# Two products change places at the head of each pass, and six idle products go before the table

## The chip, the cores and the metric

The kernel runs on one core of a Trainium2 chip. The metric is the device time of one execution in microseconds (us); of several runs the median is given. A profile is one more execution, recorded by the hardware profiler; its times count from the first instruction.

A core has five engines that run at the same time and wait for each other by semaphores: TensorE (PE in the profile, with PEld for its weight loads), VectorE (DVE), ScalarE (ACT), GpSimd (POOL) and SyncE (SP), which here issues transfers. TensorE writes to PSUM only; VectorE and ScalarE read the sums from there.

## The reference, cut to what matters

There are 128 graphs of 64 nodes with 768 features. Layer 0 is normalised, passed through a ReLU, and then a graph layer with three 768 x 768 weights is added; layer 1 is an attention layer. The change touches layer 0 alone.

```python
h = jnp.maximum(_layernorm(x, axis=-1), 0.0)
# layer 0, with adj as heads and as relations (0 or 1 here)
ctx = jnp.matmul(adj, hs @ Wadj.T + badj) / deg_c[..., None]
ctx = ctx + jnp.matmul(radj, hs @ Wrev.T + brev) / rdeg_c[..., None]
ctx = ctx + hs @ Wself.T + bself
agg = jnp.einsum('bij,bijr->bir', adj, E[rels])
rel = agg @ Wr.T + br * deg[..., None]
...                                    # the same for the reverse direction, with Wrr
x = x + ctx + rel
# layer 1
h = jnp.maximum(_layernorm(x, axis=-1), 0.0)
x = x + _L1_gnn_ref(h, adj, ...)
```

The relation part depends on x not at all: it is a count of relations per node times a small table (E times Wr and Wrr, and the biases). The kernel makes the table once and multiplies counts by it.

## The kernel before

Layer 0 goes in 32 passes (`NP`) of two row tiles of 128 rows each (`k` is 0 or 1). The products of rows and weights use a scheme for 2 x 3 by 3 x 3 blocks with 15 block products in place of 18. Each entry of `PRODUCTS` names the operand, the weight block, the PSUM bank, whether it starts that bank afresh, the block of the result, the sign, and whether counts are added as well. A product that doesn't start its bank afresh accumulates on what is in it. Pass 0 uses 18 plain products instead, while the sums of weights are being made.

```python
PRODUCTS = (
    ("f1", "g6", "a", True, "11", "+", False),
    ("f7", "g10", "b", True, "00", "-", False),
    ("a01", "b11", "d", True, "01", "+", True),
    ("f4", "b21", "a", False, "01", "-", False),
    ("a00", "g12", "b", False, "01", "-", False),
    ("f3", "g8", "c", True, "12", "-", False),
    ...
    ("a11", "g1", "b", False, "11", "+", True),
    ("f2", "g11", "a", False, "10", "+", True),
)
PLAIN = tuple((f"a{k}{j}", f"b{j}{q}", "abcdab"[2 * i + k], j == 0, f"{k}{q}" if j == 2 else None,
               "+", i > 0) for i, q in enumerate((0, 2, 1)) for k in range(2) for j in range(3))
```

A pass is a list of steps for TensorE. Each step is one fp32 matmul of the source, which the profile shows as two records; a product is six steps, so twelve records. After a product's last step VectorE adds (or subtracts) the bank to x. Each bank has one buffer.

```python
def main(p):
    ...
    def new(b):
        bank[b] = psw.tile([P, 512], F32, name=f"pw{b}")

    def counts(b, c, first=False):           # two bf16 matmuls: counts times the table
        ...
            nc.tensor.matmul(bank[b][:, :CQ], CT_T[p, k][: 3 * (e - a), i, :],       # L617
                             tabs[i][:, q * CQ : (q + 1) * CQ], ...)

    def add(b, c, sign="+"):
        ...
        if sign == "+":
            nc.vector.tensor_add(v, bank[b][:, :CQ], v)                              # L625
        else:
            nc.vector.tensor_sub(v, v, bank[b][:, :CQ])                              # L627

    def product(an, bn, b, first, c, sign, cnt):
        def step(q, s):
            if first and q == s == 0:
                new(b)
            nc.tensor.matmul(bank[b][:, :CQ], OPS[p, an][:, q, s, :],                # L633
                             bw[bn][:, (s * KQ + q) * CQ : (s * KQ + q + 1) * CQ], ...)
            if q == KQ - 1 and s == 2 and c:
                if cnt:
                    counts(b, c)
                add(b, c, sign)
        for q in range(KQ):
            for s in range(3):
                steps.append(lambda q=q, s=s: step(q, s))

    for x in PRODUCTS if p else PLAIN:
        product(*x)

    rest_of = ["12"] if p else ["00", "10"]
    for i, c in enumerate(rest_of):
        b = "dc"[i % 2]
        steps.append(lambda b=b, c=c: (counts(b, c, True), add(b, c)))
    return steps
```

Between these steps, at given places, stands the work that makes ready the next pass (and ends the one before). A few of the entries:

```python
steps = [(0, lambda: form(p, "f5", "f6", "f3")), (10, lambda: form(p, "f10")),
         (18, lambda: form(p, "f11"))]
...
    (7, lambda: prep(n)),                    # two casts of adj on VectorE
    (13, lambda: devs(n)),
    ...
    (53, lambda: form(n, "f1")),
    ...
    (66, lambda: form(n, "f7", "f4")),
```

Ahead of pass 0 the table is made and the first operands. `degrees` is a bf16 matmul with `blkb`; `table_product` is two fp32 matmuls of 384 columns (four records), of which 0 and 1 are the two directions and 2 the biases; `operands` multiplies rows of h by the adjacency divided by the degrees.

```python
prep(0)
scaled_rows()
rd = degrees(0)                              # L518
to, mv = deviations((0,))
one_over(rd)
mean_and_relu(0, to[0], mv[0])               # h of row tile 0, on ScalarE
over_degrees(0, rd)
table_product(0)                             # L458
operands(0, 0, 0)                            # L586
table_product(1)
table_product(2)
table_copy()
operands(0, 0, 1)
...
first = [
    ...
    (30, lambda: weights_sums("w", "v")),
    (34, lambda: degrees_and_norms(1)),      # VectorE reads the degrees' PSUM tile (L520)
    (38, lambda: count_t(0, 0)),             # L572
    (45, lambda: count_t(0, 1)),
    ...]
```

Of the kernel before, what the change touches and what calls it, by code (L numbers as in the profile page):

```python
# [8 lines left out]
F32 = mybir.dt.float32  # L9
# [6 lines left out]
P = 128  # L16
# [37 lines left out]
# [7 lines that stand above are left out]
    ("a02", "g14", "a", False, "00", "-", False),  # L61
    ("f9", "g9", "b", False, "02", "+", False),
# [10 lines left out]
PLAIN = tuple((f"a{k}{j}", f"b{j}{q}", "abcdab"[2 * i + k], j == 0, f"{k}{q}" if j == 2 else None,  # L73
               "+", i > 0) for i, q in enumerate((0, 2, 1)) for k in range(2) for j in range(3))
# [58 lines left out]
def kernel(  # L133
# [45 lines left out]
    nc = tc.nc  # L179
    G, N, D = x.shape  # L180
# [9 lines left out]
    NP = NT // 2  # L190
# [35 lines left out]
    def merged(main, side):  # L226

        side = sorted(side, key=lambda e: e[0])
        i = 0
        for n, step in enumerate(main):  # L230
            while i < len(side) and side[i][0] <= n:
                side[i][1]()
                i += 1
            step()
        for _, step in side[i:]:
            step()
# [41 lines left out]
    def deviation(src, to, mv):  # L278

        st = small.tile([P, 2, 6], F32, name="st")  # L280
        for i in range(2):
            nc.vector.bn_stats(st[:, i, :], src[:, i * HALF : (i + 1) * HALF])
        nc.vector.bn_aggr(mv, st.rearrange("p a b -> p (a b)"))
        ve = small.tile([P, 1], F32, name="ve")
        nc.vector.tensor_scalar(ve, mv[:, 1:2], EPS, None, op0=OP.add)  # L285
        nc.gpsimd.tensor_tensor(to[:, 0:1], ve, mhalf, op=OP.pow)  # L286
# [67 lines left out]
    with ExitStack() as px:  # L354
        wa = px.enter_context(tc.tile_pool(name="wa", bufs=1))
        work = px.enter_context(tc.tile_pool(name="work0", bufs=2))
        psw = px.enter_context(tc.tile_pool(name="psw0", bufs=1, space=bass.MemoryType.PSUM))
# [42 lines left out]
        blkb = wa.tile([P, P], BF16, name="blkb")  # L400
# [41 lines left out]
        vals = wa.tile([P, NG, N], BF16, name="vals")  # L442
# [4 lines left out]
        def scaled_rows():  # L447
            for d in range(2):
                nc.vector.tensor_mul(es[:, d, d * NV : (d + 1) * NV],
                                     et[:, d * NB + 1 : (d + 1) * NB], ids)  # L450

        def table_product(i):

            if i == 0:
                TAB["ps"] = pss.tile([P, 2, 512], F32, name="pb")
            for hf in range(2):
                s = slice(hf * HALF, (hf + 1) * HALF)
                nc.tensor.matmul(TAB["ps"][:NROW, hf, :HALF], es[:, i, :] if i < 2 else eb,  # L458
                                 wrt[i][:, s] if i < 2 else bia[:, s],
                                 start=(i == 0), stop=(i == 2))  # L460
# [52 lines left out]
        def degrees(p):  # L513


            ds = pss.tile([P, 2, 512], F32, name="pb")[:, 0, : 4 * N].rearrange(
                "p (k d n) -> p k d n", k=2, d=2)
            nc.tensor.matmul(ds, blkb, AB[p], start=True, stop=True)  # L518
            rd = work.tile([P, 2, 2, N], F32, name="rd", bufs=1)
            nc.vector.tensor_scalar(rd, ds, 1.0, None, op0=OP.max)  # L520
            return rd

        def one_over(rd):
            nc.vector.reciprocal(rd, rd)

        def over_degrees(p, rd):

            for d in range(2):
                nc.vector.tensor_mul(rts[p % 2][:, :, 1 - d, :], ADF[p][:, :, d, :], rd[:, :, d, :])
# [47 lines left out]
        def operands(p, k, q):  # L577


            t = 2 * p + k  # L580
            ps = pss.tile([P, GT, 512], F32, name="pb")
            for i in range(2):
                kb = 2 * q + i
                for g in range(GT):
                    s = slice(g * N, (g + 1) * N)
                    nc.tensor.matmul(ps[:, g, i * 3 * N : (i + 1) * 3 * N],  # L586
                                     H0[t][s, kb * P : (kb + 1) * P],
                                     rts[p % 2][s, k].rearrange("p s n -> p (s n)"),
                                     start=True, stop=True)

            a = OPS[p, f"a{k}{q}"] = (
                work.tile([P, KQ, 3, P], F32, name="oq") if (k, q) == (1, 1) else
                work.tile([P, KQ, 3, P], F32, name="op", bufs=17))
            nc.scalar.copy(a.rearrange("p h s (g n) -> p g (h s) n", g=GT),  # L594
                           ps[:, :, : 6 * N].rearrange("p g (x n) -> p g x n", n=N))
# [8 lines left out]
        def main(p):  # L604

            bank = {}
            steps = []

            def new(b):
                bank[b] = psw.tile([P, 512], F32, name=f"pw{b}")  # L610

            def counts(b, c, first=False):
                k, q = int(c[0]), int(c[1])
                if first:
                    new(b)
                for i, (a, e) in enumerate(PARTS):
                    nc.tensor.matmul(bank[b][:, :CQ], CT_T[p, k][: 3 * (e - a), i, :],  # L617
                                     tabs[i][:, q * CQ : (q + 1) * CQ],
                                     start=(first and i == 0), stop=True, skip_group_check=True)

            def add(b, c, sign="+"):
                k, q = int(c[0]), int(c[1])
                v = X[2 * p + k][:, q * CQ : (q + 1) * CQ]
# [9 lines that stand above are left out]
                    nc.tensor.matmul(  # L633
                        bank[b][:, :CQ], OPS[p, an][:, q, s, :],
                        bw[bn][:, (s * KQ + q) * CQ : (s * KQ + q + 1) * CQ],
                        start=(first and q == s == 0), stop=(q == KQ - 1 and s == 2),
                        skip_group_check=True)
# [5 lines that stand above are left out]
                    for s in range(3):  # L643
                        steps.append(lambda q=q, s=s: step(q, s))

            for x in PRODUCTS if p else PLAIN:
                product(*x)

            rest_of = ["12"] if p else ["00", "10"]
# [4 lines that stand above are left out]
# [22 lines left out]
        def deviations(ts):  # L676
            to = [small.tile([P, 2], F32, name="rn") for t in ts]
            mv = [small.tile([P, 2], F32, name="mv") for t in ts]
            for i, t in enumerate(ts):
                deviation(X[t], to[i], mv[i])  # L680
            return to, mv
# [5 lines left out]
        prep(0)  # L687
        scaled_rows()
        rd = degrees(0)
        to, mv = deviations((0,))  # L690
        one_over(rd)
        mean_and_relu(0, to[0], mv[0])
        over_degrees(0, rd)
        table_product(0)
        operands(0, 0, 0)
        table_product(1)
        table_product(2)
        table_copy()
        operands(0, 0, 1)
# [98 lines left out]
        for p in range(NP):  # L798
            merged(main(p), beside(p) if p else first)
# [436 lines left out]
```

## Time and profile before

| What | Value |
|---|---|
| Median of 3 runs | 2499.7 us (2497.94, 2499.7, 2507.48) |
| The profiled execution | 2494.1 us span, 35435 instructions |
| PE busy | 2458.7 us, 12108 instructions |
| DVE busy | 1998.9 us, 4105 instructions |
| ACT busy, POOL busy | 1074.4 us, 449.2 us |

In a line of the costliest groups the columns are: line of the kernel, engine, operation, what it writes and what it reads, the shape, how often; then, after a bar, the busy time in us and the mean of one in ns; after a second bar, the idle time of the engine ahead of these instructions and what ended most of it. In the list of waits a line says who waited for whom, for how many us in total, how many times, and the longest. In the timeline a line has the start in us, the duration in us, the engine and line, the operation, what it writes and reads, and how many are merged into it; in brackets the idle time before it and what ended it. `pwa` to `pwd` are the PSUM banks a to d of layer 0; `pb` are PSUM tiles for operands, table and degrees. Records of matmuls overlap their successors, since matmuls are pipelined: the distance of two starts says more than a duration.

### The profile page before, as it was taken

Reading aid. Unit: us, or ns where it says so; the run is one execution under the profiler, and the core shown is the slowest. Engines: PE = TensorE matmul, PEld = TensorE weight load, DVE = VectorE, ACT = ScalarE, POOL = GpSimd, SP = SyncE. Lnnn points to the kernel's source line nnn. Section 1 sums busy time; section 2 is a strip of 40 time slices with the busy share of each in tenths; the row PEclk is TensorE's granted clock in tenths of the full one; section 3 lists DMA queues with packets and bytes.
Section 4 is the critical chain, followed back from the end, with each engine's and each line's share of the span. In section 5 each row is a group of like instructions: output and inputs, shape, how many; then the busy total and the mean of one; then the engine's idle time right before and its main releaser. Section 6 shows DMA issues by size and latency. Waiting matters only on the chain. (4 is left out here: it accounts for less than half of the span.)

```text
span 2494.1 us, 35435 instructions
## 1 busy us (share of the span) xinstructions
PE 2458.7 (99%) x12108; PEld 1724.9 (69%) x12108; DVE 1998.9 (80%) x4105; ACT 1074.4 (43%) x3591; POOL 449.2 (18%) x799
## 2 busy tenths in 40 slices
PE   8999999999999999999999999999999999999997
PEld 6888888888888888888888884444444444444445
DVE  8877777777777777777777766888888888888889
ACT  2122122122122222222222224777777777777777
POOL 1112112112111121121121121111111111111122
PEclk9999999999999999999999999999999999999999
DMA  5112112112122122122122154344444444444434
GB/s 178 55 53 106 53 60 100 53 66 93 54 72 87 53 74 85 53 79 81 54 88 72 53 174 140 94 110 111 109 104 110 104 104 104 107 113 105 104 85 100
DMA packets 116215, 224.58 MB, mean 90 GB/s; under 512 B 36554, under 2 KB 49981, under 8 KB 116034
## 3 DMA queue, kind: packets, MB, share of 16 engines
q1 hardware_dynamic: 106162, 197.50, 24.4%
q0 software_dynamic: 9728, 24.78, 6.2%
q8 instruction: 95, 1.56, 0.3%
q14 instruction: 86, 0.70, 0.1%
q10 hardware_dynamic: 144, 0.04, 0.0%
HBM read 96.07 MB, written 100.66 MB: 79 GB/s over the span
## 5 line engine op out<-in xcount | busy, mean ns | idle before, releaser
L633 PE MATMUL pwa<-weights,op 128*128 128x256 f32 x2304 | 548.9, 383 | 10.6 <-DVE x L625 8.8
L633 PEld LDWEIGHTS pwa<-weights,op 128*128 128x128 f32 x2304 | 417.4, 190 | 79.3 <-DVE x L625 17.3
L633 PE MATMUL pwb<-weights,op 128*128 128x256 f32 x1536 | 360.7, 381 | 0.0
L633 PEld LDWEIGHTS pwb<-weights,op 128*128 128x128 f32 x1536 | 289.1, 190 | 44.9 <-issue 6.7
L889 PE MATMUL pma<-weights,op_f 128*128 128x512 f32 x620 | 307.7, 593 | 0.6 <-DVE weights L916 0.6
L286 POOL TENSOR_TENSOR rn<-ve,mhalf 128x1 f32<-128x1 f32 x128 | 93.7, 732 | 948.6 <-DVE ve L285 948.5
L307 DVE TENSOR_TENSOR op<-op 128x768 f32<-128x768 f32 x248 | 241.3, 993 | 1.2
L941 ACT ACTIVATE pr<-pr 128x128 f32<-128x128 f32 x768 | 225.4, 296 | 25.3 <-DVE pr L931 25.2
L483 ACT ACTIVATE h<-x,rn 128x768 f32<-128x768 f32 x64 | 62.4, 1022 | 399.8 <-DVE rn L290 380.9
L663 ACT ACTIVATE hf<-x,rn 128x768 f32<-128x768 f32 x64 | 65.7, 1027 | 353.7 <-issue 250.1
L594 ACT COPY op<-pb 128x768 f32<-128x768 f32 x160 | 121.1, 797 | 180.9 <-PE pb L586 180.3
L889 PE MATMUL pmb<-weights,op_f 128*128 128x512 f32 x372 | 191.2, 595 | 0.0
L889 PEld LDWEIGHTS pma<-weights,op_f 128*128 128x128 f32 x620 | 111.8, 190 | 113.2 <-issue 104.3
L633 PE MATMUL pwc<-weights,op 128*128 128x256 f32 x780 | 187.0, 383 | 0.0
L633 PE MATMUL pwd<-weights,op 128*128 128x256 f32 x768 | 176.3, 379 | 0.0
L633 PEld LDWEIGHTS pwc<-weights,op 128*128 128x128 f32 x780 | 145.6, 190 | 25.2 <-issue 6.7
L665 POOL TENSOR_TENSOR x<-x,hf 128x768 f32<-128x768 f32 x64 | 136.1, 2127 | 134.9 <-ACT hf L663 134.9
L633 PEld LDWEIGHTS pwd<-weights,op 128*128 128x128 f32 x768 | 145.8, 190 | 20.0 <-issue 0.2
L586 PE MATMUL pb<-r,h 64*128 64x192 f32 x1536 | 151.8, 337 | 0.4 <-ACT h L483 0.4
L625 DVE TENSOR_TENSOR x<-pwa,x 128x256 f32<-128x256 f32 x95 | 40.0, 422 | 134.2 <-PE pwa L617 78.4
L586 PEld LDWEIGHTS pb<-r,h 64*128 64x128 f32 x1536 | 122.9, 187 | 33.9 <-issue 22.7
L941 ACT ACTIVATION_READ_ACCUMULATOR pr<-pr 128x1 f32 x768 | 144.4, 188 | 0.0
(207 smaller groups left out, 4337.6 us busy)
## 6 DMA issues: line engine op xcount, KB each, us to landing
x<-in_x_dram SPq DMA_DIRECT2D x64, 384.0 KB
h<-hf SPq DMA_DIRECT2D x64, 384.0 KB
out_dram<-x SPq DMA_DIRECT2D x64, 384.0 KB
hh<-hh SPq DMA_DIRECT2D x64, 384.0 KB
h<-h SPq DMA_DIRECT2D x64, 384.0 KB
x<-hh SPq DMA_DIRECT2D x64, 384.0 KB
out_dram<-f POOLq DMA_DIRECT2D x62, 384.0 KB, 5.0
hx<-weights SPq DMA_DIRECT2D x88, 192.0 KB
```

The source lines that it names most:

```text
L286: nc.gpsimd.tensor_tensor(to[:, 0:1], ve, mhalf, op=OP.pow)
L307: return (nc.vector.tensor_add if s1 == "+" else nc.vector.tensor_sub)(to, x, y)
L483: nc.scalar.activation(h, X[t], AF.Relu, scale=to[:, 0:1], bias=to[:, 1:2])
L586: nc.tensor.matmul(ps[:, g, i * 3 * N : (i + 1) * 3 * N], H0[t][s, kb * P : (kb + 1) * P], rts[p % 2][s, k].rearrange("p s n -> p (s n)"), ...
L594: nc.scalar.copy(a.rearrange("p h s (g n) -> p g (h s) n", g=GT), ps[:, :, : 6 * N].rearrange("p g (x n) -> p g x n", n=N))
L625: nc.vector.tensor_add(v, bank[b][:, :CQ], v)
L633: nc.tensor.matmul(bank[b][:, :CQ], OPS[p, an][:, q, s, :], bw[bn][:, (s * KQ + q) * CQ : (s * KQ + q + 1) * CQ], start=(first and q == s ...
L663: nc.scalar.activation(h, X[t], AF.Relu, scale=to[:, 0:1], bias=to[:, 1:2])
L665: nc.gpsimd.tensor_add(X[t], X[t], h)
L889: nc.tensor.matmul(bank[p, b], OPS[p, an][:, q, :], bw2[bn][:, 2 * q * CQ : 2 * (q + 1) * CQ], start=(first and q == 0), stop=(q == KQ - 1 ...
L941: nc.scalar.activation(PR[t][:, j, h, :], PR[t][:, j, h, :], AF.Copy, accum_out=to)
```

## The change

In passes 1 to 30 the first two products change places: (f7, g10) in bank b comes first, and (f1, g6) in bank a second. Pass 31 keeps the old order, and pass 0 has its own products. It is meant to let the bank in which a pass ends be read out before the next pass writes it.

Ahead of the table six bf16 products of 512 columns are issued whose result nothing reads; they are there to occupy TensorE before the first products that count. The table's second direction is moved ahead of the first operands, so that TensorE has it to do while h is being made.

```diff
-            for x in PRODUCTS if p else PLAIN:
+            later = (PRODUCTS[1], PRODUCTS[0], *PRODUCTS[2:]) if p + 1 < NP else PRODUCTS
+            for x in later if p else PLAIN:
                 product(*x)
...
         prep(0)
         scaled_rows()
         rd = degrees(0)
+
+        idle = psw.tile([P, 512], F32, name="pwa")
+        for i in range(6):
+            nc.tensor.matmul(idle, blkb, vals[:, : 512 // N, :], start=True, stop=True)
         to, mv = deviations((0,))
         one_over(rd)
         mean_and_relu(0, to[0], mv[0])
         over_degrees(0, rd)
         table_product(0)
+        table_product(1)
         operands(0, 0, 0)
-        table_product(1)
         table_product(2)
         table_copy()
         operands(0, 0, 1)
```

## Prediction

> **What bounds the kernel now.** I read the page's shares and its 40 slices first, then the waits of TensorE (PE), then the timeline at the places where PE waits. The page:
>
> ```profile
> PE 2458.7 (99%) x12108; PEld 1724.9 (69%) x12108; DVE 1998.9 (80%) x4105; ACT 1074.4 (43%) x3591; POOL 449.2 (18%) x799
> L633 PE MATMUL pwa<-weights,op 128*128 128x256 f32 x2304 | 548.9, 383 | 10.6 <-DVE x L625 8.8
> ```
>
> PE is busy for 99% of the span. The change touches layer 0 alone, which ends near 1505 us (the last record of its products starts at 1504.4). What PE lost in layer 0 is in the list of waits by PE:
>
> ```profile
> PE pwa L633 <- DVE x L625: 8.8, 30, 0.3
> PE pb L518 <- DVE ab L490: 4.2, 1, 4.2
> ...
> PE pwa L633 <- DVE x L627: 1.7, 1, 1.7
> PE pb L572 <- DVE rd L520: 0.9, 1, 0.9
> ```
>
> The reader is to see that one wait comes 30 times: the first product of a pass, written to bank a, waits for VectorE (DVE) to have added bank a into x. There are 32 passes and so 31 boundaries. Here is the boundary into pass 2 (timeline):
>
> ```profile
> 118.69 0.39 PE L617 MATMUL pwa<-tab,cntT 126*128 126x256 bf16 x2
> 118.91 0.38 PE L617 MATMUL pwd<-tab,cntT 126*128 126x256 bf16 x2
> 119.11 0.42 DVE L625 TENSOR_TENSOR x<-pwa,x 128x256 f32<-128x256 f32 x1 [2.56 <-PE pwa L617]
> 119.59 2.86 PE L633 MATMUL pwa<-weights,op 128*128 128x256 f32 x12 [0.29 <-DVE x L625]
> 122.28 2.75 PE L633 MATMUL pwb<-weights,op 128*128 128x256 f32 x12
> ```
>
> The last product of a pass (f2, g11) ends in bank a with its counts at 118.69; one more pair of counts goes to bank d; then the next pass starts in bank a again, before DVE's 0.42 us read is over. All 30 such boundaries have the same figures, and passes follow each other every 46.30 us. The boundary out of pass 0, which runs the plain products and ends in bank b, has no wait:
>
> ```profile
> 72.72 0.39 PE L617 MATMUL pwb<-tab,cntT 126*128 126x256 bf16 x2
> 72.95 0.38 PE L617 MATMUL pwd<-tab,cntT 126*128 126x256 bf16 x2
> 73.17 0.39 PE L617 MATMUL pwc<-tab,cntT 126*128 126x256 bf16 x2
> 73.34 0.42 DVE L625 TENSOR_TENSOR x<-pwb,x 128x256 f32<-128x256 f32 x1
> 73.39 2.75 PE L633 MATMUL pwa<-weights,op 128*128 128x256 f32 x12
> ```
>
> The start (timeline) shows PE at two paces:
>
> ```profile
> 7.07 0.26 PEld L458 LDWEIGHTS pb<-wrt,es 128*81 128x81 f32 x1 [0.38 <-issue]
> 7.71 0.26 PEld L458 LDWEIGHTS pb<-wrt,es 128*81 128x81 f32 x1 [0.38 <-issue]
> 9.56 1.39 PE L586 MATMUL pb<-r,h 64*128 64x192 f32 x8 [0.36 <-ACT h L483]
> 11.27 0.15 PEld L458 LDWEIGHTS pb<-wrt,es 128*81 128x81 f32 x1 [0.17 <-issue]
> 11.59 0.15 PEld L458 LDWEIGHTS pb<-wrt,es 128*81 128x81 f32 x1 [0.17 <-issue]
> 14.62 1.99 PE L633 MATMUL pwa<-weights,op 128*128 128x256 f32 x8
> 39.26 0.27 PE L572 MATMUL pb<-identb,c 128*126 128x128 bf16 x2 [0.88 <-DVE rd L520]
> ```
>
> Equal table matmuls follow each other every 0.64 us at 7.1 and every 0.32 us at 11.3.
>
> **What the Trainium skill says.** "TensorE: Matmul & The Clock Gate", Part 1: the array runs at half rate by default and at full rate once a window of about 3.4 us has been busy; the window runs free, so the moment differs from run to run. The trace agrees: 0.64 us against 0.32 us, and the operand matmuls before 10.88 change pace, some 4 us after the first table matmul at 6.38. The same page gives 512 / 1.2 = 427 ns between cold bf16 matmuls of 512 columns, which I use for the six idle products; no record of the kernel before has such a matmul. "PSUM — Partial Sum Buffer", the section on bank collisions, asks for a semaphore guard by bank: the add has to be over before PE writes the same bank. That is the wait of 119.59. "Perfetto Trace Analysis", on consistent bubbles, reads a gap that repeats on the busiest engine as too few buffers; here another order of banks does what another bank would.
>
> **The change part by part.**
>
> *1. The swap, passes 2 to 30.* In these passes the product (f7, g10) in bank b comes first and (f1, g6) in bank a second. Without a wait a product follows a pair of counts after 0.22 us (72.95 to 73.17 to 73.39 are two such steps) and takes 12 x 0.216 = 2.59 us; so from the bank d counts to the second product it would be 2.81. The trace has 122.28 - 118.91 = 3.37. The loss is 0.56 us per boundary: 0.46 of a later start (0.68 instead of 0.22), and 0.10 because the weights of a waiting first matmul are not loaded ahead (2.86 against 2.75 for the twelve). The wait list shows only 0.29 of this since the end of the counts' records overlaps the gap. Bank b was last read by DVE after the product (a11, g1): counts at 115.70, add 116.13 to 116.55, 2.5 us before it would be wanted. So the wait goes entirely: passes 2 to 30 are 29 boundaries, 29 x 0.56 = 16.2 us saved.
>
> *2. The swap in pass 1.* Pass 0 ends in bank b, with the add at 73.34 to 73.76. With bank b first, PE waits for it: start at about 73.76 + 0.06 (the lag 119.53 to 119.59) = 73.82 instead of 73.39, plus 0.10 for the first matmul: 0.53 us lost. A new wait, once.
>
> *3. Pass 31* keeps the old order, so its boundary keeps its 0.56: nothing. The 1.7 us wait of its last product is in its own DVE stream and moves along with it: nothing.
>
> *4. Does the second product meet a new wait?* It needs bank a 2.81 us after the bank d counts; the add ends at 0.62 after them. The fourth product (f4) accumulates in bank a after the add of the second: PE ends the second at about 5.5 after the counts, DVE adds until about 6.0 and PE wants the bank at 8.2. Free by 2 us. DVE before that: three sums (f5, f6, f3) from 0.9 to 3.6, the first add, two casts, f10 until 5.4. Nothing new.
>
> *5. The start.* The six products read blkb and vals (both written by 3.3 us) and fill PE from about 4.5, where the degrees matmul ends, to 4.5 + 6 x 0.43 = 7.1 us (estimate). The first table product could have started at 6.38: 0.7 us later. In return, the busy stretch begins 1.9 us earlier (4.45 instead of 6.38), so the clock should come up about 8.6 instead of 10.5. Then: table products 0 and 1, eight matmuls from 7.1, two and a half at 0.64 and the rest at 0.32, end at 10.4; the second table product fills the 0.36 us in which PE waited for h (ready at 9.51); operands 0.7 more, product 2 of the table 1.3, the second operands 0.8: first product at about 13.5 instead of 14.62, 1.1 us earlier. With the free-running window this can be 0.2 (clock as late as before) to 1.9 (clock up at 7.1). The first weights have landed by then (the trace's DMA completions: 9.96, 10.68, 12.93). But what is gained must pass 39.26, where PE waits for DVE: DVE sums w and v from 35.44 to 38.87 and only then reads the degrees. v needs b21, whose DMA completions end at 36.15 whatever PE does; v now starts at about 37.15. So at most 1.0 us gets through. I take 0.75.
>
> *Sum:* -16.2 + 0.5 - 0.75 = -16.4 us. Layer 1 has the same instructions and starts when layer 0 ends: it only moves.
>
> **The rivals.** *A. DVE takes the place.* If DVE were as late as PE, only a part of the 0.56 would come through. For it: DVE is 80% busy over the span and in pass 0 nearly all the time. Against it: in the passes concerned DVE idles 2.56 us just before the last adds (119.11), so it is released by PE at each boundary and follows it. It would make the saving 5 to 10 us: 2490 to 2495. *B. The start decides.* The six products only delay the table, the clock comes no sooner, and the gain is swallowed at 39.26: start 0 to +0.7 us instead of -0.75, total 2483.5 to 2485. *C. Only the recorded gap is saved:* 29 x 0.29 = 8.5 us, about 2491. Against it: the spacing of the starts, 3.37 against 2.81, needs no end of a record. *D. A transfer becomes the limit*: x tiles come one pass ahead, and DMA is 20% busy in the middle slices; a pass shorter by 1.2% won't reach it.
>
> **Range and chances.** 2499.7 - 16.4 = 2483.3; the three times of before lie at 2497.94, 2499.7 and 2507.48, so the median stands 1.8 over the lowest and a new median could be 3 lower or 6 higher from scatter alone. The parts worked out are good to about 1.5 us. I put 2483 with 2477 to 2490. The saving is 0.66%; 2% would be 50 us, for which no wait of layer 0 is long enough, and nothing added costs that much: faster by over 2% 0.01, within 2% 0.98, slower 0.01.
>
> **What would show it.** Passes 2 to 30 every 45.74 us instead of 46.30; the wait of pwa L633 for x L625 down from 30 times to 1, a wait of the first pwb in pass 1 of about 0.5; 0.22 us from the bank d counts to a pwb product; six matmuls of about 0.43 us from 4.5; table matmuls at 0.32 us pace before 10; first pwa product near 13.5; the matmul of 39.26 near 38.4. It would be wrong if PE waited for DVE at the second or fourth product, if the passes stayed at 46.3, or if the first products waited for weights.

## The result and the profile after

The changed kernel takes 2481.48 us (median of 4 runs, 2481.21 to 2483.03), beside 2501.7 us for the kernel before (2497.94 to 2507.48, with one run more than the three above): a ratio of 0.9918, 95% interval 0.9897 to 0.9940. So it is faster by 0.8%, clear of the scatter and within 2%. The forecast was 2483.0, in a range of 2477 to 2490. The profiled execution went from a span of 2494.1 us to 2479.7.

The list of waits by PE, kernel after (who waited for whom: us in total, times, longest):

```profile
PE pwa L633 <- DVE x L627: 1.8, 1, 1.8
PE pb L572 <- DVE rd L520: 0.9, 1, 0.9
...
PE pwa L633 <- DVE x L625: 0.3, 1, 0.3
PE pwb L633 <- DVE x L625: 0.3, 1, 0.3
```

The wait that came 30 times comes once for bank a, at the head of pass 31, and once for bank b, at the head of pass 1. The timeline of the kernel after at the head of pass 2:

```profile
118.70 0.39 PE L617 MATMUL pwa<-tab,cntT 126*128 126x256 bf16 x2
118.93 0.39 PE L617 MATMUL pwd<-tab,cntT 126*128 126x256 bf16 x2
...
119.12 0.42 DVE L625 TENSOR_TENSOR x<-pwa,x 128x256 f32<-128x256 f32 x1 [2.56 <-PE pwa L617]
119.15 2.75 PE L633 MATMUL pwb<-weights,op 128*128 128x256 f32 x12
...
121.74 0.59 PE L633 MATMUL pwa<-weights,op 128*128 128x256 f32 x2
```

From the bank d counts to the first product it is 0.22 us now, and to the second 2.81 (3.37 before). VectorE's read of bank a, 119.12 to 119.54, lies beside the product in bank b, and bank a has long been free when the second product wants it at 121.74. The first weight load of the product in bank b starts at 119.04, 0.11 us ahead of its matmul; before, load and matmul of the waiting product both started at 119.59. The heads of passes follow each other every 45.74 us (118.93 and 164.67 for passes 2 and 3, and so for all up to 31), 46.30 before. The head of pass 1 in the same timeline:

```profile
72.66 0.38 PE L617 MATMUL pwc<-tab,cntT 126*128 126x256 bf16 x2
72.83 0.42 DVE L625 TENSOR_TENSOR x<-pwb,x 128x256 f32<-128x256 f32 x1
...
73.31 2.86 PE L633 MATMUL pwb<-weights,op 128*128 128x256 f32 x12 [0.26 <-DVE x L625]
```

Here the swap made a wait: 0.65 us from the last counts to the product instead of 0.22, and 2.86 for the twelve instead of 2.75. The start of the kernel after, PE alone:

```profile
4.40 2.77 PE L696 MATMUL pwa<-vals,blkb 128*128 128x512 bf16 x6
6.96 4.07 PE L458 MATMUL pb<-wrt,es 128*81 128x384 f32 x8
10.96 0.92 PE L586 MATMUL pb<-r,h 64*128 64x192 f32 x8
...
14.10 1.99 PE L633 MATMUL pwa<-weights,op 128*128 128x256 f32 x8
...
38.75 0.27 PE L572 MATMUL pb<-identb,c 128*126 128x128 bf16 x2 [0.88 <-DVE rd L520]
```

The six idle products take 0.43 us each; the clock record puts full rate at 9.62 us (10.55 before). The first product comes 0.52 earlier than the 14.62 of before, and the matmul behind VectorE 0.51 earlier than 39.26.

So layer 0 gained what was worked out. By the 1446.06 of the first product of pass 31 (1462.29 before) the kernel was 16.23 us ahead, and so it stayed through layer 1 until its last 35 us. There it lost 1.8. Two windows of the kernel before (stretch in us, its length, then busy time and records of PE, PEld, DVE, ACT and POOL, the granted PE clock, DMA share, GB/s):

```profile
2468.00:2478.00 10.00, 5.23 (x33) 3.59 (x25) 9.72 (x22) 7.56 (x38) 2.47 (x7) 0.85 0.57 127
2478.00:2488.00 10.00, 5.33 (x63) 3.97 (x61) 9.39 (x28) 6.00 (x18) 3.21 (x3) 0.98 0.48 65
```

The stretch from the same point of the program in the kernel after, which is 16.2 us ahead there:

```profile
2452.00:2462.00 10.00, 5.23 (x23) 3.72 (x20) 9.71 (x22) 7.27 (x36) 2.47 (x7) 0.75 0.59 127
2462.00:2472.00 10.00, 7.31 (x63) 5.53 (x63) 8.03 (x25) 5.38 (x18) 2.06 (x2) 0.74 0.31 45
```

PE waits here for other engines, and the clock drops: for 3.41 us in the kernel before, for 10.24 in the kernel after. The same four matmuls in the chain of work that ended last (start, us), first before and then after:

```profile
2478.97 1.06 PE pma L1099 x4
```

```profile
2463.55 2.00 PE pma L1106 x4
```

With the clock at half they take about twice as long, VectorE waits for them (8.03 busy instead of 9.39), and the program ends later. Whether the change did that was the first question for the experiments.

### The profile page after: what moved, and what is told of

The parts are those of the page before. It is cut to its first block, busy times and chain, and to the rows that moved or that the text cites. A ratio compares the mean times of both kernels' runs of the same rounds, so it can differ in the third digit from the quotient of the medians.

```text
span 2479.7 us, 35447 instructions
## 1 busy us (share of the span) xinstructions
PE 2455.0 (99%) x12114; PEld 1727.4 (70%) x12114; DVE 1999.0 (81%) x4105; ACT 1074.7 (43%) x3591; POOL 450.1 (18%) x799
```

## The experiments

Each was run beside the kernel before on the same chip. The table has the traces' own times in us: the start of the first product; from it to the first product of pass 31; from there to a fixed VectorE instruction in layer 1 (the 1300th record from the end); from another (the 200th from the end) to the end of the span. Between those two lie 615.08 us in every one of them.

| Kernel | first product | to pass 31 | into layer 1 | last part | span |
|---|---|---|---|---|---|
| before, first profile | 14.62 | 1447.67 | 313.69 | 103.03 | 2494.1 |
| before, again | 14.45 | 1447.71 | 314.75 | 105.05 | 2497.0 |
| before, third | 14.36 | 1447.67 | 314.79 | 104.93 | 2496.8 |
| before, fourth | 16.66 | 1447.67 | 316.68 | 105.31 | 2501.4 |
| swap alone | 14.59 | 1431.96 | 313.83 | 104.71 | 2480.2 |
| start alone | 12.86 | 1448.41 | 315.51 | 105.41 | 2497.3 |
| changed kernel | 14.10 | 1431.96 | 313.76 | 104.81 | 2479.7 |
| swap from pass 2 | 14.11 | 1431.44 | 313.90 | 104.83 | 2479.3 |
| swap in pass 31 too, loads as they were | 13.17 | 1431.83 | 318.32 | 103.84 | 2482.2 |
| idle products alone | 14.31 | 1447.66 | 314.16 | 104.61 | 2495.8 |
| table moved alone | 15.17 | 1447.66 | 316.00 | 104.86 | 2498.8 |
| swap from pass 2, idle products at the end | 13.02 | 1432.01 | 315.88 | 102.81 | 2478.8 |
| and swap in pass 31, one load later | 13.62 | 1431.00 | 314.35 | 102.80 | 2476.8 |
| and idle products earlier | 12.91 | 1431.47 | 314.50 | 103.07 | 2477.0 |

**The kernel before again.** No edit.

> The kernel before, once more, to see how far its own times and its two ends scatter. My theory (the clock window runs free of the program): passes again every 46.30 us, 30 boundaries with 0.68 us from the bank d counts to the next product; the clock comes up at another moment than 10.55 us, anywhere from 9.8 to 13.2, and the last 35 us of the program have a stretch at half clock of one or more windows of 3.41 us. Rival (the change itself cost the 1.8 us at the end of the program): the kernel before always has just one window of 3.41 us at half clock in its last 35 us, as in its first profile.

Median 2499.01 of 12 runs, ratio to the kernel before 0.9995 (0.9985 to 1.0006), as it should be. Passes 46.30 us, clock up at 10.35. The windows near the end:

```profile
2469.00:2479.00 10.00, 5.23 (x26) 3.64 (x18) 9.71 (x22) 7.26 (x36) 2.48 (x7) 0.79 0.59 127
2479.00:2489.00 10.00, 7.74 (x63) 5.96 (x63) 7.81 (x24) 5.07 (x18) 2.06 (x2) 0.70 0.32 48
```

The kernel before has the half clock near its end as well, 10.24 us of it from 2474.78, and its last part takes 105.05. The rival falls: the kernel without the change loses them too, here and in its third and fourth profile (104.93 and 105.31). The first profile of before, at 103.03, was a lucky one.

**The swap alone.** The start as before:

```diff
-        idle = psw.tile([P, 512], F32, name="pwa")
-        for i in range(6):
-            nc.tensor.matmul(idle, blkb, vals[:, : 512 // N, :], start=True, stop=True)
...
-        table_product(1)
         operands(0, 0, 0)
+        table_product(1)
```

> The swap without the changed start. My theory: passes 2 to 30 every 45.74 us, a new wait of 0.53 us in pass 1, so the first product of pass 31 starts 15.7 us (29 x 0.56 - 0.53) earlier than in a kernel before whose start is the same; about 0.5 us later than in the changed kernel. Rival (the two parts help each other, the swap needs the earlier start): the first product of pass 31 comes over 1 us later than 15.7 says.

Median 2486.01 of 4 runs (2481.94 to 2490.82), ratio 0.9940 (0.9922 to 0.9958). From the first product to pass 31 it takes 1431.96 us, to the hundredth what the changed kernel takes, and 15.71 less than before: 29 x 0.56 - 0.53 = 15.71. Up to pass 31 the swap needs nothing of the start. The timed runs say less: the median lies 14.3 us under the kernel before beside it and 4.5 over the changed kernel (timed apart), where 0.5 was expected, and the four runs are spread over 8.9 us. Only the fastest of them was profiled, so what held up the others, and whether the new start prevents it, is not shown.

**The start alone.** `for x in PRODUCTS if p else PLAIN` as before, the rest as changed.

> The start without the swap. My theory: the passes stay at 46.30 us; the first product comes 0.2 to 1.2 us earlier than 14.62, by the phase of the clock window, and at most 1.0 of it passes the wait for VectorE at 39 us; over the whole kernel 0.2 to 1.0 us, too little to be seen in the medians. Rival (the six products only delay the table): first product at 14.6 or later.

Median 2498.43 of 12 runs, ratio 0.9991 (0.9983 to 1.0000). The clock was up at 7.11 us and the first product at 12.86, 1.8 us before that of the kernel before, more than the 0.2 to 1.2 expected; of this 1.0 was left at pass 31 (1461.27), and nothing at the end, as pass 31 and the last part took 1.8 and 2.4 us longer than in the first profile of before. The timeline of VectorE shows where the rest stayed:

```profile
33.69 1.76 DVE L307 TENSOR_TENSOR weights<-weights 128x1536 f32<-128x1536 f32 x1
36.09 1.76 DVE L307 TENSOR_TENSOR weights<-weights 128x1536 f32<-128x1536 f32 x1 [0.65 <-DMA tab<-tl]
37.77 0.42 DVE L520 TENSOR_SCALAR rd<-pb 128x256 f32<-128x256 f32 x1
```

These are w and v. In the kernel before v followed w at once; here VectorE waits 0.65 us for a transfer. The profile names another transfer that ended at that time; by the program the one that v needs is b21. The completion that let v go came at 35.87; the same one came at 36.15 in the first profile of before and at 35.36 in the second, so the cap itself moves by some tenths. PE stands behind it until 38.24. That is the cap that was expected.

**The swap from pass 2 on.**

```diff
-            later = (...) if p + 1 < NP else PRODUCTS
+            later = (...) if 1 < p < NP - 1 else PRODUCTS
```

> The changed kernel with the old order in pass 1, so that passes 2 to 30 alone are swapped. My theory: the wait of the first product of pass 1 goes and nothing takes its place, so from pass 1 on everything is 0.53 us earlier than in the changed kernel (if its start falls alike). Rival (VectorE sets the pace out of pass 0, where it is nearly always busy): the 0.53 us comes back as a wait later in pass 1 and the first product of pass 2 starts at the same time as in the changed kernel.

Median 2483.05 of 4 runs (2481.13 to 2485.27), ratio 0.9928 (0.9913 to 0.9943). The timeline at the head of pass 1:

```profile
72.67 0.39 PE L617 MATMUL pwc<-tab,cntT 126*128 126x256 bf16 x2
72.89 2.75 PE L633 MATMUL pwa<-weights,op 128*128 128x256 f32 x12
```

The wait is gone, and pass 31 comes 0.52 us sooner after the first product than in the changed kernel (1431.44). Nothing took its place. The medians can't show half a microsecond; the trace does.

**The swap in pass 31 too.** `... if p else PRODUCTS`, nothing else.

> The changed kernel with the swap in the last pass too. Theory one (the last pass is bound by VectorE and by the loads of layer 1's weights, not by PE): the wait of 0.56 us at the head of pass 31 goes, but (f1, g6) is now read second, so the first load that overwrites g6 starts 2.6 us later; the wait of the pass's last product for VectorE, 1.8 us in the changed kernel, grows by 0.6 to 3.2 us and layer 0 ends at the same time or up to 2.6 us later. Theory two (the wait at the head is on the path in pass 31 as in the others): layer 0 ends 0.56 us earlier and the last product's wait stays at 1.8.

Both theories missed. In pass 31 the load of b10 for layer 1 goes into the place of g6 and is issued after the first of the second product's six steps. That product now reads g6 from there: its other five steps wait for the load and multiply b10's numbers, so this kernel leaves most of the product with g6 out of pass 31. PE, kernel with the swap in all passes:

```profile
1447.59 0.59 PE L633 MATMUL pwa<-weights,op 128*128 128x256 f32 x2
1451.00 4.10 PE L633 MATMUL pwa<-weights,op 128*128 128x256 f32 x10 [2.82 <-DMA weights<-in_w_cat_dram]
1454.89 2.81 PE L633 MATMUL pwd<-weights,op 128*128 128x256 f32 x12
```

A wait of 2.82 us, and then ten records in 3.9 us instead of 2.2, since the clock fell to half from 1451.58 to 1454.99. Median 2485.58, ratio 0.9939 (0.9926 to 0.9953). That the change spares pass 31 fits this; what the wait at its head is worth it does not tell.

**The two parts of the start, each alone.** Idle products without the move of the table, and the move without the idle products; products in the old order in both.

> The six idle products alone: old order of products, table's second direction in its old place. In the timed runs of the kernel before about a third lie 5 to 6 us over the rest (near 2504 instead of 2498); with the whole new start none of twelve does. Theory one (the idle products bring the clock up early whatever the window's phase): no run near 2504, median within 1 us of the start-only kernel's 2498.4. Theory two (moving the table is what helps, since PE no longer waits for h): about a third of the runs near 2504. First product in the trace between 13.4 and 15.3 in both.

> The table's second direction ahead of the first operands, without the idle products. Theory one (the idle products are what removes the slow third of the runs): some of the runs near 2504 again, median 2499 to 2502. Theory two (moving the table is what helps): no run near 2504, median within 1 us of 2498.4. In the trace table matmuls start near 6.4 and the wait for h is gone in both.

Idle products alone: median 2499.11 of 13 runs (2496.57 to 2501.62), ratio 0.9992 (0.9984 to 1.0000); clock up at 8.93, first product at 14.31, and PE still waits 0.32 us for h. The move alone: median 2500.16 of 13 (2498.30 to 2502.20), ratio 0.9997 (0.9988 to 1.0005); clock up at 12.16, first product at 15.17. The medians order them as theory one says, and the idle products alone have no run near 2504. But the move alone has none either, which theory one did not expect. Neither part has a gain in its median that its interval sets apart from nothing; what can be seen is that runs over 2503 are gone with either of them (of 26 none; of the 25 timed beside them of the kernel before 7).

**A run near 2504, caught.** The kernel before, two more profiled executions.

> The kernel before, looked at once more, to catch one of its executions near 2504 us (17 of 60 timed ones were at 2503 or more; none of 38 with any part of the new start). Theory one (the start): the clock comes up late or the first products wait, and the first product of pass 31 starts some 5 us after 1462.2. Theory two (the passes fall into another rhythm): the passes are longer than 46.30 us by about 0.2. Theory three (the end): all is as before until 1462, and the 5 us are lost in pass 31 or in the last 35 us. If this execution is again near 2498, it says nothing of the three.

> The same kernel and the same three theories as in the run before it: a second chance to catch an execution near 2504 us.

(Of the 60 times meant there 18 are at 2503 or more, not 17.) The first took 2498.60 us, the second 2503.17. The start of the second, PE:

```profile
9.65 1.65 PE L586 MATMUL pb<-r,h 64*128 64x192 f32 x8 [0.36 <-ACT h L483]
11.23 2.85 PE L458 MATMUL pb<-wrt,es 128*81 128x384 f32 x4
...
16.66 1.99 PE L633 MATMUL pwa<-weights,op 128*128 128x256 f32 x8
```

The table matmuls at 11.23 still run at half rate (2.85 us for four against 1.52): the clock came up at 14.76, and pass 31 began 2.04 us later than in the first profile. In pass 31:

```profile
1505.26 4.43 PE L633 MATMUL pwa<-weights,op 128*128 128x256 f32 x12 [3.07 <-DVE x L627]
```

The last product waited 3.07 us for VectorE instead of 1.75, and then took 4.43 instead of 2.86, as the clock was at half from 1506.38 to 1509.80. The last part lost another 2.3 against the first profile. So here theories one and three hold together, and theory two falls: the passes are 46.30 us. Beside the execution of 2498.60, a more usual one, the 4.6 us are 2.3 at the start, 1.9 in pass 31 and 0.4 in the last part; the start alone is less than the 5 us of theory one. Whether all runs near 2504 are of this kind stays open: many of them have a mean granted clock of 0.997, and this one 0.996.

**Idle products in the last waits of PE.** On the kernel with the swap from pass 2:

```diff
         PS[t] = pss.tile([P, 512], F32, name="ps")
+        if t == NT - 1:
+            for _ in range(20):
+                nc.tensor.matmul(PS[t][:, : N + P], idr[:, N:], idr, start=True, stop=True)
         nc.tensor.matmul(PS[t][:NR, : N + P], sdb[...], idr, start=True, stop=True)
```

and 24 more of them in the same way ahead of the last tile's logits.

> The changed kernel with the old order in pass 1, and 44 idle bf16 products of 192 columns in the two waits of PE (1.9 and 2.3 us) in the last row tile, written to the PSUM tile that the product after them overwrites. Theory one (the stretch at half clock near the end, 10.24 us in the changed kernel, comes from windows in which PE is mostly idle): no or a later drop of the clock before PE's last matmul, end of the kernel 1 to 2 us earlier than the same kernel without them. Theory two (the end is bound by VectorE and the clock is a bystander): same time, within 0.3 us, from layer 1's last 35 us on; or slower by what the idle products take.

Timeline of PE in this kernel:

```profile
2454.95 1.81 PE L975 MATMUL ps<-idr 128*128 128x192 bf16 x20
2457.00 0.28 PE L976 MATMUL ps<-idr,sdb 128*82 128x192 bf16 x1 [0.24 <-POOL sdb L959]
2457.11 2.14 PE L995 MATMUL ps<-idr 128*128 128x192 bf16 x24
2459.59 0.32 PE L997 MATMUL ps<-rrow,lrow 82*128 82x384 bf16 x1 [0.33 <-DVE rrow L980]
```

Its windows from the same point of the program:

```profile
2453.00:2463.00 10.00, 8.13 (x88) 6.95 (x83) 9.71 (x22) 7.63 (x38) 2.48 (x7) 1.00 0.61 126
2463.00:2473.00 10.00, 4.75 (x54) 3.39 (x45) 9.61 (x28) 5.95 (x18) 3.21 (x3) 0.93 0.54 68
```

The idle products fill the waits and are over before the next operand comes. The clock stays at full rate until 2471.59, after PE's last matmul, VectorE is busy for 9.61 us of a stretch in which it was busy for 8.03 in the changed kernel, and the last part takes 102.81 us instead of 104.83. Theory one holds, with 2.0 us. What the idle products gain hangs on where the half clock falls without them: the three traces that have them show 102.80 to 103.07, the eleven others 103.03 to 105.41, and the 103.03 is the profile with only 3.41 us at half clock. Median 2480.33, ratio 0.9920 (0.9907 to 0.9934).

**Both ends, and pass 31 with a later load.** The same, with the swap in pass 31 and the load of b10 after step 12:

```diff
-            later = (...) if 1 < p < NP - 1 else PRODUCTS
+            later = (...) if p > 1 else PRODUCTS
...
-                    (7, "b10"), (13, "b00"), ...
+                    (13, "b10"), (13, "b00"), ...
```

> The kernel with idle products at the end (old order in pass 1), with the swap in pass 31 as well and the load of b10 issued after step 12 instead of step 6, so that the second product still reads g6. Theory one (in pass 31 the path runs through the loads of layer 1's weights, which are issued by steps of PE): the 0.56 us at the head goes, the loads issued after it are 0.56 earlier too, and the last product's wait for VectorE stays between 1.7 and 3.1, so layer 0 ends 0.56 us earlier after the head of pass 31. Theory two (the loads are bound by the transfers themselves, not by their issue): the last product's wait grows by the 0.56 us. Whole kernel: 2479 to 2481, under the 2481.5 of the changed kernel.

> The same with 16 idle products of 128 columns ahead of the degrees matmul and 5 of 512 behind it, so that PE is busy from 2.4 us on. Theory one (the clock comes up after the first clock window that is busy throughout): clock up between 5.8 and 9.2 us instead of 7.2 to 11, but the loss at 38 to 39 us behind VectorE caps the gain, so the first product of pass 2 starts at 117.9 to 118.2 in every trace and the median is 0 to 0.5 us under the run beside it. Theory two (the idle products before the degrees delay VectorE, which reads the degrees): later by up to 0.5 us.

The first: median 2478.62 of 5 runs, ratio 0.9922 (0.9909 to 0.9936), the lowest span of all, 2476.8. The head of pass 31, PE:

```profile
1444.39 0.39 PE L617 MATMUL pwd<-tab,cntT 126*128 126x256 bf16 x2
1444.62 2.75 PE L633 MATMUL pwb<-weights,op 128*128 128x256 f32 x12
```

The wait at the head is gone. Whether the gain survives to the end of the pass stays open: the last product waited 2.52 us, within the 1.7 to 3.1 that this wait has had in all traces, so the two theories can't be told apart. Against the changed kernel's trace it is 2.9 us shorter: 0.5 of an earlier clock, 1.0 of the heads of passes 1 and 31, 2.0 of the end, less 0.6 in pass 31. These two kernels were not timed beside each other.

The second, with PE busy from 2.36 us: clock up at 6.02, median 2478.59 of 4 runs, ratio 0.9920 (0.9906 to 0.9933), and pass 2's first product at 117.93, 0.23 us before the run beside it, though the first product was 0.7 earlier. The cap behind VectorE holds; no delay by the idle products shows.

## Why the prediction was right, point by point

*The swap in passes 2 to 30 (16.2).* Right: the swap alone gives 15.71 with pass 1 taken off. The loss was read off the distance of starts; the 0.29 us that the wait list shows would have given half of it (rival C). That the recorded gap is short since the counts' records run on beyond the next start fits the 0.39 us records at 0.22 us distance.

*Pass 1 (0.53).* Right: 0.52 by the kernel that leaves it out.

*No new wait at the second or fourth product, VectorE follows PE (rival A).* Right: the wait list has none, VectorE still idles 2.56 us ahead of the last adds, and each pass gave 0.56. No wait of PE for a transfer came up either (rival D).

*The start (0.75, at most 1.0).* Right in kind, too simple about the clock. In the changed kernel's trace it was 0.51, and the clock came up at 9.62, not 8.6. The forecast moved the rise by the 1.9 us by which the busy stretch begins earlier. But the window that ended at 6.21, counted back from the rise by 3.41 us, was busy for 58% only; the next one, busy throughout, brought the clock up. The forecast's pieces add up to 13.2 for the first product, not the 13.5 it gives: the steps behind the table took 3.14 us and not the 2.8 of the sum. The rest of the way to 14.10 is the table's eight matmuls, which took 4.00 us instead of the estimated 3.3 under the later clock. The cap was seen in the trace of the start alone, where 1.8 us earlier at the first product left 1.0. The six products did not cost their delay (rival B). What the estimate didn't have is the scatter of the other side: the first product of the kernel before came at 14.36 to 16.66 in four traces.

*Pass 31 and layer 1 only move.* This was too simple. The wait of the last product is 1.7 to 3.1 us from trace to trace: VectorE waits there for the last weights of layer 1 (1.33 us in the first profile, 2.36 in the second, ahead of the same sum). And the stretches at half clock in pass 31 and in the last 35 us come and go with the window. The change touches neither, but they are what makes the times differ by some microseconds. From the first profile of before to that of after the kernel gained 16.2 up to its last 35 us and gave 1.8 back there; against the second profile of before it gained 17.3. By the medians it gained 20.2: the kernel before also has runs up to 2507, and the four of the changed kernel lie within 1.8 us. What the fourth trace of before lost accounts for some of this surplus of some 4 us over the forecast; whether the rest is scatter or the new start sparing the changed kernel slow runs is not shown. The forecast's ratio 2483.0 / 2499.7 = 0.9933 lies in the measured interval. That the 2483.0 came so close to the median is in part luck, since the 2499.7 it was reckoned from stood at 2501.7 in the comparison; the gains read off the traces, stage by stage, are what bears the forecast out.

## What to carry to other kernels

A gap on the busiest engine that comes once per pass was worth its excess in the distance of starts times the passes here, since no other engine was as late; and another order of work removed it without another buffer. To try it elsewhere, start with the bank that was read out longest ago, and look at the first and last pass by themselves, since their neighbours differ. Count a gain at the start only up to the next wait for something that doesn't move, here a transfer. On TensorE, idle products in a wait that can't be removed are worth trying where matmuls at half clock would follow on the path; see that they end before the operand comes.

## What was not expected of the hardware

All stretches at half clock in the middle of the program are 3.41 us or two or three times that, and the moments at which the clock changes lie on one grid of 3.41 us within a trace but not from trace to trace. This fits the free-running window of the Trainium skill ("TensorE: Matmul & The Clock Gate", Part 1). But a wait much shorter than a window was enough to lose one: 1.89 us in pass 31 of the start-alone kernel, whose clock was then at half from 1502.15 to 1505.57. PE was busy for 45% of the window ahead of it. A longer wait at the same place, 2.80 us in the second profile of before, lost none: it lay across the end of a window at 1501.98. Yet the window up to there was busy for only 43%, so the busy share by the records does not settle it either. And PE busy for most of a window did not always suffice to raise it: 62% did not (table moved alone, the window before 8.75), 84% did (start alone, the window before 7.11), and in the trace near 2504 a window with 0.36 us of idle time did not (the one before 11.34), though one with as much did in the first profile of before (the one before 10.55). The operands' 64-row matmuls fill about half of the first and less than a third of the second. That rows count in this is a guess; no run tested it.
